# Layer 0 of a two-layer transformer block: biases in one piece, experts' first tokens loaded three waves ahead, small steps moved into gaps, copies behind products

## The chip, the cores and the metric

The kernel runs on one core of a Trainium2 chip. Its engines work from queues of their own and meet only through semaphores: TensorE (PE, matrix products and transposes, with a separate track for loading weights, PEld), VectorE (DVE), ScalarE (ACT), GpSimd (POOL) and SyncE (SP, which here only issues DMA transfers). DMA transfers are also issued from ACT's and POOL's queues. The metric is the device time of one execution in microseconds; the number compared is the median of the runs.

## What is computed

The input x has 8 sequences of 512 tokens with 256 features, in float32. Two layers follow each other.

```python
x = layernorm(x + attention0(x))      # 16 heads of 16, softmax over keys j >= i
x = layernorm(x + experts0(x))        # 8 experts, top 2; the last one only scales x;
                                      # 7 have 256 -> 1024 -> relu -> 256, at most 512 tokens each
x = layernorm(x + attention1(x))      # RMS norm, rotary positions, sigmoid weights
x = layernorm(x + experts1(x))        # 8 experts 256 -> 512 -> silu -> 256, and 4 that only scale x; top 2
```

Each query, key and value is a product of x with a 256x256 matrix plus a bias. Experts of layer 0 take the first 512 tokens that chose them, in the order of the tokens.

## The kernel before, in words

The kernel keeps all sequences in SBUF (`own[b]`, 128 partitions x 4 x 256) and writes one instruction stream by hand. Inside `tc.manual_schedule()` the order of the source is the order on each engine; outside it, as in `layer0()`, where weights and constants are loaded, a scheduler places the instructions.

**Start.** `layer0()` loads the first sequence, the query and key weights (`unspread`, L262, pieces of 16 floats), and the two biases. A bias of 256 numbers comes from the host as 128 x 4, where only 16 of every 32 partitions hold data. `packed` (L254) brings it into the layout of the products, 128 x 2, with eight small DMA transfers; the query's eight go out on SP's queue and the key's eight on ACT's queue. DVE then builds `bq_t` and `bk_t` (L400 to L402). `turned_in(0, kc)` (L466, L469) transposes the first sequence on PE in two halves, with one copy on ACT after each. Both halves use the one PSUM buffer that `bank()` gives in this layer, so the second half's transposes wait for the first copy. `query` (L499, L506) then multiplies by the weights.

**Waves.** `waves0(start, stop)` runs attention in steps called waves, 16 for each sequence. Each wave computes scores of four heads for one block of keys, their exponentials on ACT, a mask on POOL, and the products with the values; beside these it runs the small steps that `beside0` lists for that wave, for the sequence before and the one after. In the waves of sequence 6 the rows of sequence 4 are scattered into `xbuf`, two of the last eight in each of waves 8 to 11 (L764, indirect DMA on POOL's queue). Only sequences 0 to 4 are scattered here; a flag says later whether experts had room left, and a second pass follows if so.

**Experts of layer 0.** After the 112 waves of sequences 0 to 6, `experts0` runs the seven experts, and then the waves of the last sequence follow. Two experts' weights are loaded long before. `tokens0(e)` (L1333, SP's queue) loads an expert's 512 rows from `xbuf` into a tile of the pool tag "e", which has five buffers and also holds the exponentials of the waves. `turn(e)` (L1350) transposes them into a two-bank PSUM tile of `wide()`, of which there are three, and DVE and ACT copy one half each (L1354, L1355). Four groups of products follow (L1368), each with a relu copy on ACT or DVE, then four output blocks of eight products (L1385). All four blocks lie in one PSUM tile of two banks; after the second block DVE copies the first bank (L1392), after the fourth ACT copies the second (L1394). Then SP stores the result and loads weights and tokens of expert e+2.

**Steps in gaps.** 37 small steps of attention are left at that point: four transposes back to token order of sequence 6 (`by_token`, L589, with a reciprocal and a multiplication on DVE, L595 and L598), four query or key products of sequence 7 (`query`), then `by_feature`, `kept`, `projected` and the routing. They stand in a list; `gap()` runs the next one. Before the first `turn(0)` eight are run in a row, four `by_token` and four `query` in turn, all through the single buffer of `bank()`. The rest are run in the gaps of the experts, of which there are seven for each expert and six for the last.

Of the kernel before, what the change touches and what calls it, by code (L numbers as in the profile page):

```python
# [9 lines left out]
FP = mybir.dt.float32  # L10
# [7 lines left out]
P = 128  # L18
B, S, D = 8, 512, 256
NT = B * S  # L20
KC = D // P
NC = S // P
NH, HD = 16, 16
NHS = 4
# [19 lines left out]
def tile_two_layers(  # L44
# [33 lines left out]
    nc = tc.nc  # L78
# [5 lines left out]
    p = {}  # L84
# [11 lines left out]
    def bank():  # L96
        return p["mm"].tile([P, 512], FP, tag="mm", name="mm")


    ident = const.tile([P, P], FP, name="ident")  # L100
# [6 lines left out]
        out=before, in_=ones, pattern=[[1, P]], compare_op=ALU.is_gt, fill=0.0,  # L107
# [35 lines left out]
    for i, (seqs, always) in enumerate(LOTS):  # L143
        n = seqs * S
        lot = SimpleNamespace(
            i=i, first=len(lot_of), n=n, slots=E1 * n, always=always, most=2 * n // TB + E1 - 1
# [97 lines left out]
    def packed(pool, src, n, name, queue=nc.sync):  # L244

        t = pool.tile([P, KC, n], FP, name=name)
        unspread_rows(t, src, queue)
        return t
# [9 lines left out]
    def unspread(pool, src, name, queue=nc.sync):  # L258

        t = pool.tile([P, KC, NH, HD], FP, name=name)  # L260
        for kc in range(KC):
            queue.dma_start(  # L262
                out=t[:, kc],
                in_=src[kc * P : (kc + 1) * P, :].rearrange("p (h x) -> p h x", x=32)[:, :, :HD],
            )
        return t.rearrange("p k h x -> p k (h x)")
# [78 lines left out]
    att = work.enter_context(tc.tile_pool(name="att", bufs=1))  # L345
    alone = ExitStack()
    wp = alone.enter_context(tc.tile_pool(name="w0", bufs=1))
# [10 lines left out]
    def pair(name):  # L358
        return att.tile([P, 2, S], FP, tag="e", name=name, bufs=5)

    def layer0():
        def load_x(b):
            nc.sync.dma_start(out=own[b], in_=x[b].rearrange("(c p) d -> p c d", p=P))

        st = [{} for _ in range(B)]
        load_x(0)
        wq_s = unspread(wp, wq0, "wq_s")
        wk_s = unspread(wp, wk0, "wk_s", nc.scalar)
        bq_s = packed(wp, bq0.unsqueeze(2), 1, "bq_s")
        bk_s = packed(wp, bk0.unsqueeze(2), 1, "bk_s", nc.scalar)  # L370

        wv_s = wp.tile([P, KC, D + 8], FP, name="wv_s")
        nc.sync.dma_start(out=wv_s[:, :, :D], in_=wv0.rearrange("(k p) f -> p k f", p=P))
# [25 lines left out]
        for m in range(KC):  # L399
# [9 lines left out]
            out=shade[:, :P], in_=shade[:, :P], pattern=[[1, P]], compare_op=ALU.is_ge, fill=MASKED,  # L409
# [882 lines left out]
    def waves0(start, stop):  # L1292
        nonlocal waiting
        t = l0
        for g in range(start, stop):
            b, w = g // 16, g % 16
            now = None
            if g >= 0:
                now = t.scores(b, w // 8, w // 4 % 2, NC - 1 - w % 4)
                if w % 4 == 0:  # L1300
                    t.fill(b, w // 4)
                if w == 10 and b + 2 < B:
                    t.load_x(b + 2)
            if (g + 2) % 4 == 0 and 0 <= g + 2 < 16 * B:
                ob, ow = (g + 2) // 16, (g + 2) % 16
                t.lowered(ob, ow // 8, ow // 4 % 2)
            first, second = beside0(b, w if g >= 0 else g)
            if b == 0 and w in (1, 3, 4, 5, 8, 9):
                fn, arg = t.rsteps.pop(0)
                fn(arg)  # L1310
            if b == 2 and w < len(l1.steps):
                fn, arg = l1.steps[w]
                fn(arg)
            run(first)
            ob, ow = (g + AHEAD) // 16, (g + AHEAD) % 16
            if ob < B:
                t.greatest(ob, ow // 8, ow // 4 % 2, (1, 0, 3, 2)[ow % 4])
            if waiting:
                t.gathered(*waiting)
            run(second)  # L1320
            waiting = now
# [6 lines left out]
        nc.sync.dma_start(out=wo, in_=we_out[e].rearrange("(f p) d -> p f d", p=P))  # L1328
        return wi, wo

    def tokens0(e):
        xe = pair(f"xe{e}").rearrange("p u (c d) -> p (u c) d", d=D)
        nc.sync.dma_start(  # L1333
            out=xe, in_=xbuf[e * CAP : (e + 1) * CAP, :].rearrange("(c p) d -> p c d", p=P)
        )
        return xe

    def experts0(loaded, h, steps):

        xes = {e: tokens0(e) for e in range(2)}  # L1340

        def gap():
            if steps:
                run([steps.pop(0)])

        def turn(e):
            ps = wide()
            for kc in range(KC):
                for c in range(NC):
                    nc.tensor.transpose(  # L1350
                        ps[:, kc, c * P : (c + 1) * P], xes[e][:, c, kc * P : (kc + 1) * P], ident
                    )
            xeT = pair(f"xeT{e}")
            nc.vector.tensor_copy(xeT[:, 0, :], ps[:, 0, :])  # L1354
            nc.scalar.copy(xeT[:, 1, :], ps[:, 1, :])  # L1355
            return xeT

        for _ in range(8):
            gap()
        xeT = turn(0)  # L1360
        for e in range(E0):
            wi, wo = loaded[e]
            for f2 in range(I0 // P // 2):
                ps = wide()
                for u in range(2):
                    f = 2 * f2 + u
                    for kc in range(KC):
                        nc.tensor.matmul(  # L1368
                            out=ps[:, u, :], lhsT=wi[:, kc, f * P : (f + 1) * P], rhs=xeT[:, kc, :],
                            start=(kc == 0), stop=(kc == KC - 1),  # L1370
                        )
                for u in range(2):
                    if f2 % 2 == 0:
                        nc.scalar.activation(h[2 * f2 + u], ps[:, u, :], AF.Relu)
                    else:
                        nc.vector.tensor_scalar(h[2 * f2 + u], ps[:, u, :], 0.0, None, ALU.max)
                gap()
            if e + 1 < E0:
                xeT = turn(e + 1)
                gap()  # L1380
            ps = wide().rearrange("p u (c d) -> p (u c) d", d=D)
            ye = pair(f"ye{e}").rearrange("p u (c d) -> p (u c) d", d=D)
            for c in range(NC):
                for f in range(I0 // P):
                    nc.tensor.matmul(  # L1385
                        out=ps[:, c, :], lhsT=h[f][:, c * P : (c + 1) * P], rhs=wo[:, f, :],
                        start=(f == 0), stop=(f == I0 // P - 1),
                    )
                if c % 2 == 0:
                    gap()  # L1390
                elif c == 1:
                    nc.vector.tensor_copy(ye[:, :2, :], ps[:, :2, :])  # L1392
                else:
                    nc.scalar.copy(ye[:, 2:, :], ps[:, 2:, :])  # L1394
            nc.sync.dma_start(
                out=ybuf[e * CAP : (e + 1) * CAP, :].rearrange("(c p) d -> p c d", p=P), in_=ye
            )
            if e + 2 < E0:
                loaded[e + 2] = weights0(e + 2)
                xes[e + 2] = tokens0(e + 2)  # L1400
        run(steps)
# [128 lines left out]
    loaded = {}  # L1530
    with tc.manual_schedule():
        for kc in range(KC):
            l0.turned_in(0, kc)
        for which in ("q", "k"):
            for part in range(2):
                l0.query(0, 0, which, part, lambda: wide()[:, 0, :])
        waves0(-AHEAD, 32)
        l1 = layer1(att.tile([P, KC, S], FP, tag="aoT", name="turns"))
        waves0(32, 48)
        for e in range(2):  # L1540
            loaded[e] = weights0(e)
        waves0(48, 16 * (B - 2))
        h = [half(f"h{f}") for f in range(I0 // P)]
        waves0(16 * (B - 2), 16 * (B - 1))
        l0.gathered(*waiting)
        waiting = None
        a, z, n = B - 2, B - 3, B - 1
        t = l0
        steps = [(t.by_token, a, 0), (t.query, n, 1, "q", 0), (t.by_token, a, 1), (t.query, n, 1, "q", 1)]
        steps += [(t.by_token, a, 2), (t.query, n, 1, "k", 0), (t.by_token, a, 3), (t.query, n, 1, "k", 1)]  # L1550
        steps += [(t.by_feature, a, kc) for kc in range(KC)]
        steps += [(t.kept, z, c) for c in (2, 3)]
        steps += [(t.projected, a, c) for c in range(NC)]
        steps += [(fn, z) for fn in (t.chosen, t.raised, t.shared, t.pointed, t.counted)]
        steps += [(t.filled,)]
        steps += [(fn, z) for fn in (t.ranked, t.sent)]
        steps += [(fn, a) for fn in (t.normed, t.logits)]
        steps += [(t.kept, a, c) for c in range(NC)]
        steps += [
            (fn, a) for fn in (t.chosen, t.raised, t.shared, t.pointed, t.counted, t.ranked, t.sent)  # L1560
        ]
        experts0(loaded, h, steps)
    moe0.close()
    planp = ctx.enter_context(tc.tile_pool(name="planp", bufs=1, side="right"))
    rows1 = ExitStack()
# [432 lines left out]
```

## Time and profile before

| | |
|---|---|
| median of 3 runs | 1585.18 us (1585.05 to 1585.28) |
| profiled execution | 1617.07 us, its span 1615.4 us |
| mean granted TensorE clock | 0.944 |
| busy in the span | PE 1456.2 us, DVE 903.9, ACT 675.9, POOL 479.5 |
| first query product | at 15.49 us |
| last products of the 112 waves | end at 571.2 us |
| first `turn(0)` transpose, first expert product | 593.93 us, 596.70 us |
| last expert product | ends at 808.2 us |

The profile is that of one execution, which was 2.0% longer than the median of the runs. In its lines a time is the start in microseconds from the beginning of the span, followed by the duration; the bracket at the end says how long the engine had been idle before and what released it. "SPq" and "ACTq" are DMA issues of these engines' queues. A float32 product appears as two PE records, a transpose as one. Some PE records are missing from the trace, so counts there are a lower bound.

### The profile page before, as it was taken

Reading aid. Unit: us, or ns where it says so; the run is one execution under the profiler, and the core shown is the slowest. Engines: PE = TensorE matmul, PEld = TensorE weight load, DVE = VectorE, ACT = ScalarE, POOL = GpSimd, SP = SyncE. Lnnn points to the kernel's source line nnn. Section 1 sums busy time; section 2 is a strip of 40 time slices with the busy share of each in tenths; the row PEclk is TensorE's granted clock in tenths of the full one; section 3 lists DMA queues with packets and bytes.
Section 4 is the critical chain, followed back from the end, with each engine's and each line's share of the span. In section 5 each row is a group of like instructions: output and inputs, shape, how many; then the busy total and the mean of one; then the engine's idle time right before and its main releaser. Section 6 shows DMA issues by size and latency. Waiting matters only on the chain. (4 is left out here: it accounts for less than half of the span.)

```text
span 1615.4 us, 24867 instructions
## 1 busy us (share of the span) xinstructions
PE 1456.2 (90%) x8558; PEld 773.1 (48%) x8558; DVE 903.9 (56%) x3443; ACT 675.9 (42%) x1001; POOL 479.5 (30%) x602
## 2 busy tenths in 40 slices
PE   5999889898989879999998999999999999999992
PEld 3444444444443336666633333333333333778882
DVE  3655667676767532321073656767767665453394
ACT  2544444453544321111043655656665656222242
POOL 2221233232323300000044303435445422432453
PEclk8999999999999979999988988999998999999996
DMA  8949950000000002233010001022012004557774
GB/s 194 284 142 356 355 168 15 10 15 12 13 12 11 4 27 78 79 115 119 13 47 21 27 2 27 26 27 39 26 25 42 19 3 132 173 170 233 260 241 155
DMA packets 136364, 150.01 MB, mean 93 GB/s; under 512 B 29869, under 2 KB 119242, under 8 KB 136226
## 3 DMA queue, kind: packets, MB, share of 16 engines
q1 hardware_dynamic: 118242, 121.63, 24.0%
q0 software_dynamic: 10560, 23.51, 5.8%
q10 hardware_dynamic: 7424, 3.15, 0.8%
q8 instruction: 72, 1.18, 0.3%
q14 instruction: 66, 0.54, 0.1%
HBM read 77.01 MB, written 77.10 MB: 95 GB/s over the span
## 5 line engine op out<-in xcount | busy, mean ns | idle before, releaser
L967 ACT ACTIVATE e<-sc 128x1024 f32<-128x1024 f32 x256 | 248.8, 1022 | 163.0 <-PE sc L959 150.6
L561 POOL TENSOR_SCALAR_AFFINE_SELECT e<-e 128x256 f32<-128x256 f32 x256 | 103.8, 413 | 629.2 <-ACT e L558 626.6
L530 DVE CUSTOM_DVE_ANT_0 seen<-sc,shade 128x128 f32<-128x128 f32 (+3 forms) x512 | 250.7, 490 | 62.0 <-PE sc L522 32.9
L558 ACT ACTIVATE e<-sc 128x1024 f32<-128x1024 f32 (+3 forms) x256 | 168.8, 702 | 99.0 <-PE sc L549 88.7
L549 PE MATMUL sc<-q,k 32*128 32x512 f32 (+3 forms) x1024 | 137.2, 506 | 10.9 <-DVE mpad L530 9.9
L976 PE MATMUL av<-e,v 128*32 128x512 f32 x1024 | 143.8, 634 | 0.0
L522 PE MATMUL sc<-k,q 32*128 32x384 f32 (+3 forms) x1024 | 131.4, 514 | 9.5 <-ACT e L558 5.0
L573 PE MATMUL av<-e,v 128*32 128x512 f32 (+3 forms) x1024 | 101.6, 467 | 4.0 <-POOL e L561 3.6
L1385 PE MATMUL sc<-wo,h 128*128 128x256 f32 x448 | 100.5, 381 | 4.8 <-DVE ye L1392 4.8
L1677 PE MATMUL yp<-w_e,h 128*128 128x256 f32 x416 | 96.5, 384 | 3.0 <-DVE h L1669 2.1
L1368 PE MATMUL sc<-xeT,wi 128*128 128x512 f32 x224 | 98.1, 593 | 0.9 <-DVE xeT L1354 0.9
L1661 PE MATMUL sc<-xtT,w_e 128*128 128x256 f32 x416 | 94.3, 380 | 0.3 <-issue 0.3
L1385 PEld LDWEIGHTS sc<-wo,h 128*128 128x128 f32 x448 | 84.0, 190 | 19.3 <-DVE ye L1392 7.9
L959 PE MATMUL sc<-q,k 16*128 16x512 f32 x512 | 84.3, 668 | 6.7 <-ACT e L967 3.2
L549 PEld LDWEIGHTS sc<-q,k 32*128 32x128 f32 x1024 | 52.7, 190 | 73.8 <-issue 42.7
L1677 PEld LDWEIGHTS yp<-w_e,h 128*128 128x128 f32 x416 | 79.7, 193 | 14.9 <-DVE h L1669 2.5
L1688 POOL DMA_INDIRECT ybuf<-yt,to x52 | 51.0, 980 | 114.5 <-DVE yt L1687 103.4
L959 PE MATMUL sc<-q,kb 32*128 32x512 f32 x512 | 80.6, 649 | 4.6 <-ACT e L967 4.6
L1661 PEld LDWEIGHTS sc<-xtT,w_e 128*128 128x128 f32 x416 | 77.2, 190 | 10.1 <-issue 0.5
L522 PEld LDWEIGHTS sc<-k,q 32*128 32x128 f32 x1024 | 53.8, 195 | 54.1 <-issue 21.1
L1142 POOL DMA_INDIRECT xbuf<-x,idx x64 | 68.0, 1062 | 23.8 <-issue 15.5
L506 ACT ACTIVATE q<-mm,bq_t,lanes 128x256 f32<-128x256 f32 x60 | 30.6, 561 | 103.1 <-PE mm L499 103.1
(287 smaller groups left out, 2166.6 us busy)
## 6 DMA issues: line engine op xcount, KB each, us to landing
xbuf<-blank SPq DMA_DIRECT2D x130, 272.0 KB
w_e<-in_w SPq DMA_DIRECT2D x104, 256.0 KB
ybuf<-blank SPq DMA_DIRECT2D x16, 512.0 KB
y<-ybuf SPq DMA_DIRECT2D x16, 512.0 KB
wi<-in_we_in SPq DMA_DIRECT2D x7, 1024.0 KB
wo<-in_we_out SPq DMA_DIRECT2D x7, 1024.0 KB
xt<-xbuf SPq DMA_DIRECT2D x26, 272.0 KB
own<-in_x SPq DMA_DIRECT2D x8, 512.0 KB
```

The source lines that it names most:

```text
L522: nc.tensor.matmul(out=places[r], lhsT=q["q", m, t][32 * r : 32 * r + 32, ib * P : (ib + 1) * P], rhs=q["k", m, t][32 * r : 32 * r + 32, i ...
L530: nc.vector.tensor_tensor_reduce(out=seen[:, :width], in0=places[r], in1=shade[:, :width], scale=-1.0, scalar=-MASKED, op0=ALU.add, op1=AL ...
L549: nc.tensor.matmul(out=places[r], lhsT=q["k", m, t][32 * r : 32 * r + 32, jb * P : (jb + 1) * P], rhs=q["q", m, t][32 * r : 32 * r + 32, : ...
L558: nc.scalar.activation(e[:, :, :width], s[:, :, :width], AF.Exp, scale=SCALE)
L561: nc.gpsimd.affine_select(out=own, in_=own, pattern=[[0, 2], [-1, P]], compare_op=ALU.is_ge, fill=0.0, base=0, channel_multiplier=1,)
L573: nc.tensor.matmul(out=q["av"][32 * r : 32 * r + 32, : (jb + 1) * P], lhsT=vs[b % 2][:, jb, 8 * m + 2 * r + t, :], rhs=es[r], start=(jb == ...
L959: nc.tensor.matmul(out=scs[r // 2][:, r % 2, :], lhsT=k[32 * r : 32 * r + lanes, jb * P : (jb + 1) * P], rhs=q["q", m][32 * r : 32 * r + l ...
L967: nc.scalar.activation(e, scs[pr], AF.Sigmoid, scale=SCALE)
L976: nc.tensor.matmul(out=q["av"][32 * r : 32 * r + 32, :], lhsT=vs[b % 2][:, jb, 8 * m + 2 * r + t, :], rhs=es[r // 2][:, r % 2, :], start=( ...
L1385: nc.tensor.matmul(out=ps[:, c, :], lhsT=h[f][:, c * P : (c + 1) * P], rhs=wo[:, f, :], start=(f == 0), stop=(f == I0 // P - 1),)
L1661: nc.tensor.matmul(out=ps[:, f // 2, f % 2 * TB : (f % 2 + 1) * TB], lhsT=q.wi[kc][:, f * P : (f + 1) * P], rhs=q.xtT[:, kc, :], start=(kc ...
L1677: nc.tensor.matmul(out=q.ps[c], lhsT=q.h[:, f // 2, at : at + P], rhs=q.wo[f // 2][:, f % 2 * D : (f % 2 + 1) * D], start=(f == 0), stop=( ...
```

## The change

Four things are changed, all in layer 0.

1. The two biases are each loaded with one DMA transfer on SP's queue, as they come (128 x 4), into `spread`. DVE copies the right columns of the identity matrix into `lane`, and two products on PE with `lane` as weights put the numbers in the layout of the products. DVE copies the result from PSUM to `biases`. The eight DMA transfers on SP's queue and the eight on ACT's queue are gone. The order that the scheduler gives puts the two new products at the head of PE's queue, ahead of the first transposes, and they use the buffer of `bank()` that the transposes need next; on SP's queue the two loads stand between the first sequence and the query weights.
2. The first two experts' tokens are loaded three waves before the end of sequence 6, into one tile of the tag "o" (two buffers), instead of after the last wave into two tiles of the tag "e".
3. `turn(0)` comes first; then two steps instead of eight are run before the first expert; the other 35 go into the 48 gaps.
4. Both copies of an expert's output stand behind all four blocks of products.

```diff
         load_x(0)
+        spread = wp.tile([P, 2, NHS], FP, name="spread")
+        for i, src in enumerate((bq0, bk0)):
+            nc.sync.dma_start(out=spread[:, i, :], in_=src)
+        wk_s = unspread(wp, wk0, "wk_s", nc.scalar)
         wq_s = unspread(wp, wq0, "wq_s")
-        wk_s = unspread(wp, wk0, "wk_s", nc.scalar)
-        bq_s = packed(wp, bq0.unsqueeze(2), 1, "bq_s")
-        bk_s = packed(wp, bk0.unsqueeze(2), 1, "bk_s", nc.scalar)
+        lane = wp.tile([P, NHS, HD], FP, name="lane")
+        nc.vector.tensor_copy(lane, ident.rearrange("p (g x) -> p g x", x=32)[:, :, :HD])
+
+        ps = bank()[:, : 2 * KC].rearrange("p (i m) -> p i m", m=KC)
+        for a in range(2):
+            nc.tensor.matmul(
+                out=ps[64 * a : 64 * a + 64],
+                lhsT=lane.rearrange("p g x -> p (g x)"),
+                rhs=spread.rearrange("p i (m a) -> p i m a", a=2)[:, :, :, a],
+                start=True, stop=True,
+            )
+        biases = wp.tile([P, 2, KC, 1], FP, name="biases")
+        nc.vector.tensor_copy(biases.rearrange("p i m o -> p i (m o)"), ps)
+        bq_s, bk_s = biases[:, 0], biases[:, 1]
...
-    def tokens0(e):
-        xe = pair(f"xe{e}").rearrange("p u (c d) -> p (u c) d", d=D)
+    def tokens0(e, xe=None):
+        if xe is None:
+            xe = pair(f"xe{e}").rearrange("p u (c d) -> p (u c) d", d=D)
...
-    def experts0(loaded, h, steps):
-
-        xes = {e: tokens0(e) for e in range(2)}
+    def experts0(loaded, xes, h, steps):
...
-        for _ in range(8):
+        xeT = turn(0)
+        for _ in range(2):
             gap()
-        xeT = turn(0)
...
                 if c % 2 == 0:
                     gap()
-                elif c == 1:
-                    nc.vector.tensor_copy(ye[:, :2, :], ps[:, :2, :])
-                else:
-                    nc.scalar.copy(ye[:, 2:, :], ps[:, 2:, :])
+            nc.vector.tensor_copy(ye[:, :2, :], ps[:, :2, :])
+            nc.scalar.copy(ye[:, 2:, :], ps[:, 2:, :])
...
-        waves0(16 * (B - 2), 16 * (B - 1))
+        waves0(16 * (B - 2), 16 * (B - 1) - 3)
+
+        xe = att.tile([P, 2, 2, S], FP, tag="o", name="xe", bufs=2)
+        xes = {
+            e: tokens0(e, xe[:, e].rearrange("p u (c d) -> p (u c) d", d=D)) for e in range(2)
+        }
+        waves0(16 * (B - 1) - 3, 16 * (B - 1))
...
-        experts0(loaded, h, steps)
+        experts0(loaded, xes, h, steps)
```

## The prediction

> **What bounds the kernel now.** I read the page's busy times first: PE is busy for 90% of the span, the next engine for 56%.
>
> ```profile
> PE 1456.2 (90%) x8558; PEld 773.1 (48%) x8558; DVE 903.9 (56%) x3443; ACT 675.9 (42%) x1001; POOL 479.5 (30%) x602
> ```
>
> So PE's idle time is what can be won, and any PE work added where PE is busy is paid in full. Next the timeline of the start (start, duration, engine, line).
>
> ```profile
> 4.88 9.03 ACTq L254 DMA_DIRECT2D bk_s<-in_bk  x8
> 5.50 1.09 PE L466 MATMUL mm<-ident,own 128*128 128x128 f32 x4 [5.50 <-DMA own<-in_x]
> 5.76 8.48 SPq L254 DMA_DIRECT2D bq_s<-in_bq  x8
> 13.95 0.59 ACT L469 COPY xT<-mm 128x512 f32<-128x512 f32 x1 [11.86 <-DMA bk_s<-in_bk]
> 14.59 1.12 PE L466 MATMUL mm<-ident,own 128*128 128x128 f32 x4 [8.00 <-ACT xT L469]
> 15.49 3.81 PE L499 MATMUL sc<-xT,wq_s 128*128 128x256 f32 x8
> 15.74 0.59 ACT L469 COPY xT<-mm 128x512 f32<-128x512 f32 x1 [1.21 <-PE mm L466]
> ```
>
> The first transposes are done at 6.6, but ACT, which must copy them, is issuing the key bias's eight transfers until 13.9. The second copy ends at 16.33, and only then can query products be completed. The DMA view of 8 to 12 us (40 slices of 0.1 us) tells when the weights are there at the latest:
>
> ```profile
> DMA  8989999999999999922220000000000000110000
> ```
>
> The engines are full until 9.7 us. Now the hand-over to the experts, from the timeline of 571 to 600 us:
>
> ```profile
> 576.58 2.04 PE L499 MATMUL mm<-xT,wq_s 128*128 128x256 f32 x4 [3.01 <-DVE ao L598]
> 578.66 1.02 ACT L506 ACTIVATE q<-mm,bq_t,lanes 128x256 f32<-128x256 f32 x2 [5.47 <-PE mm L499]
> 579.74 1.11 PE L589 MATMUL mm<-ident,o 128*128 128x128 f32 x4 [1.11 <-ACT q L506]
> 581.75 2.04 PE L499 MATMUL mm<-xT,wq_s 128*128 128x256 f32 x4 [0.90 <-DVE ao L598]
> ...
> 593.93 1.92 PE L1350 MATMUL sc<-ident,xe 128*128 128x128 f32 x8
> 596.70 3.70 PE L1368 MATMUL sc<-xeT,wi 128*128 128x512 f32 x8 [0.85 <-DVE xeT L1354]
> ```
>
> Eight steps go through one PSUM buffer, product, copy, product, copy, at half clock: the table by stage has 12.23 us of PE in the 22 us from 572 to 594, at a granted clock of 0.58, against 39.15 of 40 at 1.00 from 600 to 640. Last, the output blocks, where PE waits for DVE's copy of a bank that it has finished:
>
> ```profile
> 617.53 3.62 PE L1385 MATMUL sc<-wo,h 128*128 128x256 f32 x16
> 621.25 0.69 DVE L1392 COPY ye<-sc 128x512 f32<-128x512 f32 x1 [2.42 <-PE sc L1385]
> 621.99 3.72 PE L1385 MATMUL sc<-wo,h 128*128 128x256 f32 x16 [0.85 <-DVE ye L1392]
> ```
>
> And SP's waits, for the tokens:
>
> ```profile
> SPq L1333 <- DMA xbuf<-own,idx_all: 340.5, 1, 340.5
> SPq L1333 <- PE av L573: 11.8, 2, 8.7
> ```
>
> **What the Trainium skill says.** "TensorE: Matmul & The Clock Gate", section "What's actually happening": the array falls to half clock after an idle window of about 3.4 us and returns after about as long of sustained work. The trace agrees: the query of two products (four records) takes 2.04 us in the stretch above and 1.13 at 544.24. "DMA: Bandwidth & Descriptors", section "Issuing engines are not separate DMA queues": transfers from SP and ACT share the same engines, so moving biases from ACT's queue saves issue time only; the trace agrees, in that both weights, one on each queue, share the engines until about 9.7 us. The same page, section "Queues, rings and completion order": each engine consumes a queue's descriptors in ring order; so the bias loads, issued right behind the first sequence and ahead of the query weights, need not wait for these. No run here shows it yet.
>
> **Part 1, the start.** Removed: eight issues (9.03 us) from ACT's queue, eight (8.48 us) from SP's. Added on SP: two issues, 0.43 each by the nearest row (bo_c, 128x2, at 17.20), which put the query weights' issue 0.9 later, hidden because their data waits behind the first sequence's. Now PE's head waits for the biases. The first sequence was there at 5.50; I take 5.9 for the biases (bounds 5.5, in the same breath, and 7.5, some 2 us behind). Two tiny products 0.3 (estimate from 0.27 for one transpose), DVE's copy 0.15 (as the 128x8 copy L491), hand-overs 0.25: 6.6. Transposes 1.09, copy 0.59, transposes 1.12, copy 0.59 and four hand-overs of some 0.03 to 0.1: 10.2. The weights: full engines until 9.7, of which the removed small loads were part, plus 0.7 for the semaphore: 10.4 (bounds 9.7 and 11.5). The later of the two decides: 10.4 instead of 16.4, **6.0 us** (bounds 4.9 and 6.4). The lane copy on DVE (0.15) runs while DVE is idle. Is something else late then? The value bias was issued at 16.18 and needed at 22.01; it moves to about 11.1 (SP was held by the query weights until 8.8) and is needed at 16. The zero fills behind it start 5 to 6 earlier as well, so they meet the same waves.
>
> **Part 2, tokens early.** The last scatter had arrived at 567.44 - 8.7 = 558.7; from there SP waited only for buffers of tag "e". In the new place both loads go out at once, with nothing else on SP's queue until the first expert's store. The old load's data moved from 568.4 to 570.6, so `turn(0)` at 571.3 would have found its tokens anyway within a microsecond: this part alone I price at 0 (bounds 0 and 1); what it does is let part 3 be safe.
>
> **Part 3, steps in gaps.** Wave products end at 571.2. `turn(0)` takes 1.04 at full clock (the row at 611.42), `by_token` stands behind it. DVE is late: its queue of maxima and logits ends at 575.73; then xeT 0.69, reciprocal and multiplication 0.74, so the query starts at about 577.3 (576.58 before, plus 0.69), half clock, 2.04: 579.3. Expert 0's products follow at once. They start cold: 1.4 lost (bounds 0 and 3.4), against 0.27 lost before (3.70 against 3.43). So 596.97 becomes 580.7: 16.3 won. Paid back: six steps now stand in PE's full stream. Four transposes there cost 0.44 (the next product after 604.11 starts at 604.55), a query 0.87 (four records; 16 records of 256 columns take 3.45): 3 x 0.44 + 3 x 0.87 = 3.9. One hand-over is tight: `by_token` right behind `turn(1)`, about 0.3, since ACT needs 1.02 for the query's copy and `turn(1)` covers 1.0. Elsewhere 3.4 us of products cover each copy. 35 steps fit in 48 gaps. **12.1 us** (bounds 9 and 14). The flag that SP reads moves to the sixth gap of expert 2; SP needs it before that expert's store, and PE needs nothing from SP for 20 us after.
>
> **Part 4, copies.** 617.53 + 3.45 = 620.98 is when the third block could start; it starts at 621.99: 1.0 for each of seven experts, **7.1 us** (5.9 by the wait of 0.85, 7.9 by PEld's waits). DVE's copy now runs beside ACT's; the PSUM tile is needed again two product groups later, 7 us, so nothing waits; the store is 0.1 later at the most.
>
> **Sum.** 6.0 + 12.1 + 7.1 = 25.2 us of the span of 1615.4. The profiled execution (1617.07) is 2.0% longer than the median, so I scale by 0.98: 24.7, and 1585.2 - 24.7 = **1560.5**. After 808 us PE stays the bound, with no wait for a DMA in the list, so the shift should last to the end.
>
> **Rivals.**
> - *The start gives nothing* (weights or biases land late, or the time is lost to fills): 19.2 x 0.98 = 18.8, 1566.4. For it: the weights' landing is inferred. Against it: DMA is quiet after 10 us. Chance 0.13.
> - *Steps stall in the gaps* as they do now: six times the 0.9 to 1.1 of the rows above, about 6: 1566.4. For it: still one buffer. Against it: 3.4 us of cover. Chance 0.10.
> - *More is won*: half clock shortened. From 29.9 to 41 us products also run at double length (2.13, 2.07); if the earlier start spares that stretch, some 6 more, and the cold 1.4: 1553. Chance 0.12.
> - *Slower: the clock.* If PE's new rhythm made it fall to half clock where it is now full, each cold microsecond costs half. To end slower by 0.2% it must lose 28 us, 56 us of extra half clock, four times the stretch at the start; in the experts the profile shows 1.00 throughout. 1590, chance 0.03.
> - *Nothing*: a wait behind the experts absorbs all, 1585. No such wait is in the list. Chance 0.02.
>
> **How the numbers follow.** The forecast itself has 0.60, with its own range of 1556 to 1565 from the bounds. The range of 8 in 10 reaches to the neighbours: 1553 to 1568. A difference within 0.2% (3.2 us) could not be told from none: faster 0.95, the same 0.02, slower 0.03.
>
> **What would show it.** ACT's first copy near 7.7 and complete query products near 10.4, no longer 16.4; the first expert product at 573 to 574 in the new span (579.3 less 6.0), no eight steps ahead; no wait of L1400 for DVE's copy; the distance from the first expert product to the last (211.5 before) about 3 shorter: 7.1 won, 4.2 paid back. Wrong would be: PE's head waiting past 8 us, gaps with idle PE in expert 0, or half clock in the experts.

## The result

The changed kernel takes 1562.2 us (median of 4 runs, 1560.8 to 1563.08), the kernel before 1585.23 (4 runs). The ratio is 0.9861, with a 95% interval of 0.9847 to 0.9875: 23.0 us or 1.4% faster. Forecast were 1560.5 us, 24.7 faster.

On the page after, the first part says that PE is the bound as before. Its busy time is shorter than the 1456.2 us of the first profile before, but most of that is a long layer 1 in that profile; a second profile of the kernel before (below) has 1432.3:

```profile
PE 1427.1 (92%) x8562; PEld 765.6 (49%) x8562; DVE 908.3 (58%) x3445; ACT 675.9 (43%) x1001; POOL 479.0 (31%) x602
```

The timeline of the start, PE's lines and then ACT's (start, duration, engine, line, and in brackets the idle time before and its releaser):

```profile
6.91 0.38 PE L377 MATMUL mm<-spread,lane 128*64 128x4 f32 x4 [6.91 <-DMA spread<-in_bk]
7.59 1.09 PE L481 MATMUL mm<-ident,own 128*128 128x128 f32 x4 [0.30 <-POOL mpad L431]
9.35 1.12 PE L481 MATMUL mm<-ident,own 128*128 128x128 f32 x4 [0.68 <-ACT xT L484]
10.26 3.81 PE L514 MATMUL sc<-xT,wq_s 128*128 128x256 f32 x8
...
8.71 0.59 ACT L484 COPY xT<-mm 128x512 f32<-128x512 f32 x1 [6.62 <-PE mm L481]
10.50 0.58 ACT L484 COPY xT<-mm 128x512 f32<-128x512 f32 x1 [1.21 <-PE mm L481]
```

PE now waits for the biases at its head, until 6.91. ACT copies as soon as PE is done, and the second copy ends at 11.08 instead of 16.33. (The bracket at 7.59 names a POOL memset that ends at 7.57, but the wait is for DVE's copy of the biases out of the same PSUM buffer, which ends at 7.49: in p1_biases below, the memset ends at 7.57 again, the copy at 7.59, and the transposes start at 7.70, so they follow the copy by about 0.1 us in both.)

PE's timeline from the last wave products into the first expert, and then an expert's output blocks:

```profile
566.38 0.86 PE L588 MATMUL av<-e,v 128*32 128x256 f32 x16
567.17 1.09 PE L1365 MATMUL sc<-ident,xe 128*128 128x128 f32 x8
...
573.24 2.04 PE L514 MATMUL mm<-xT,wq_s 128*128 128x256 f32 x4 [3.60 <-DVE ao L613]
575.07 5.22 PE L1383 MATMUL sc<-xeT,wi 128*128 128x512 f32 x8
580.13 0.60 PE L604 MATMUL mm<-ident,o 128*128 128x128 f32 x4
...
599.13 7.07 PE L1400 MATMUL sc<-wo,h 128*128 128x256 f32 x32
```

The chain of eight steps is gone; one wait of 3.60 is left in which DVE finishes its maxima. The first expert's eight products take 5.22 instead of 3.70, since about half of them run at half clock. The second and third output block are one uninterrupted row of 32 records; before, DVE's copy stood between them.

Where the time went can be laid out along four places that all kernels have. The last copy of attention output of sequence 6 marks the end of the waves; from there to the last expert product is the experts' stretch. A second profile of the kernel before (below) is used, because the first one had a long layer 1.

| | before, again | after |
|---|---|---|
| query products can be completed | 16.2 us | 11.1 us |
| second copy of attention output (sequence 0) | 79.52 | 71.76 |
| end of the waves | 572.24 | 568.69 |
| last expert product | 807.84 | 785.78 |
| experts' stretch | 235.6 | 217.1 |

So the start gives 5 to 8 us, of which some 4 are left at the end of the waves, and the experts' stretch gives 18.5.

### The profile page after: what moved, and what is told of

Same layout as the page of the kernel before. It is cut to its first block, busy times and chain, and to the rows that moved or that the text cites. A ratio compares the mean times of both kernels' runs of the same rounds, so it can differ in the third digit from the quotient of the medians.

```text
span 1559.6 us, 24858 instructions
## 1 busy us (share of the span) xinstructions
PE 1427.1 (92%) x8562; PEld 765.6 (49%) x8562; DVE 908.3 (58%) x3445; ACT 675.9 (43%) x1001; POOL 479.0 (31%) x602
## 5 line engine op out<-in xcount | busy, mean ns | idle before, releaser
L991 PE MATMUL av<-e,v 128*32 128x512 f32 x1024 | 138.3, 612 | 0.0
L974 PE MATMUL sc<-q,k 16*128 16x512 f32 x512 | 79.1, 659 | 3.9 <-PEq L1600 2.3
L974 PE MATMUL sc<-q,kb 32*128 32x512 f32 x512 | 77.3, 640 | 0.4 <-ACT e L982 0.4
```

Of the source, the lines that this page charges most:

```text
L974: nc.tensor.matmul(out=scs[r // 2][:, r % 2, :], lhsT=k[32 * r : 32 * r + lanes, jb * P : (jb + 1) * P], rhs=q["q", m][32 * r : 32 * r + l ...
L991: nc.tensor.matmul(out=q["av"][32 * r : 32 * r + 32, :], lhsT=vs[b % 2][:, jb, 8 * m + 2 * r + t, :], rhs=es[r // 2][:, r % 2, :], start=( ...
```

## The experiments

In all of them the ratio is to the kernel before, run on the same chip.

**The kernel before once more.** No edit. The spans of the first profiles before and after differ by 55.8 us while the medians differ by 23.0, so one of them isn't typical.

> The kernel before, unchanged, profiled once more, because its first profile (1617.07 us) lies 32 us above its runs. Theory (the change acts in layer 0 alone): this execution is near 1585 us, the experts' stretch from the end of the wave products to the last expert product is again 237 us, and layer 1's waves, 400 us in the first profile, take about 375 as in the changed kernel, because those 25 us were half clock in that one execution. Rival (the change shortens layer 1 too): layer 1's waves take about 400 us again.

It took 1582.69 us. The first and last score product of layer 1 are seen in the list of the instructions of that line, in the first profile and in the second (minimum, median and maximum duration in ns, then first and last start in us):

```profile
L959 PE MATMUL sc<-q,k x512: 587/692/1218, 871.6 to 1361.8; 16*128 16x512 f32 x171
```

```profile
L959 PE MATMUL sc<-q,k x512: 587/692/1218, 871.2 to 1332.6; 16*128 16x512 f32 x171
```

Up to layer 1 both are alike within 0.5 us; then the first needs 490.2 us, the second 461.4, as the changed kernel does (461.6). Of the 34.4 us between the two spans these waves of layer 1 make 28.8 (about 25 were expected), and most of the rest comes behind them; the change has no part in them. The clock accounts for most of it: in these stretches PE was busy for 469.2 and 447.9 us with the same 2746 records, at a granted clock of 0.94 and 0.98. The experts' stretch is 235.6, close to the 237 expected.

**Each part alone.** From the kernel before, one part of the diff each.

```diff
# p1_biases: only the loads, the two products and the copy of the biases
# p2_tokens: only waves0(..., 16 * (B - 1) - 3), the tile of the tag "o", and tokens0(e, xe)
# p3_steps
-        for _ in range(8):
+        xeT = turn(0)
+        for _ in range(2):
             gap()
-        xeT = turn(0)
# p4_copies
                 if c % 2 == 0:
                     gap()
-                elif c == 1:
-                    nc.vector.tensor_copy(ye[:, :2, :], ps[:, :2, :])
-                else:
-                    nc.scalar.copy(ye[:, 2:, :], ps[:, 2:, :])
+            nc.vector.tensor_copy(ye[:, :2, :], ps[:, :2, :])
+            nc.scalar.copy(ye[:, 2:, :], ps[:, 2:, :])
```

> Part 1 alone: biases loaded in one piece each and ordered by two products; all else as before. Theory (the start's gain stays): 6 us faster than before, 1579; complete query products at about 11.1 us instead of 16.4. The changed kernel stood 8.0 us ahead at the first sequence's end and 3.9 ahead at the end of the wave products; theory: that is the clock's coming and going, so here the lead at the end of the waves may be anything from 3 to 9 and PE's granted clock in the waves explains the difference. Rival (the waves give the start's gain back, fills and loads meeting them at a worse place): 4 us or less, and the lead falls between 150 and 571 us at the same waves at the same granted clock.

> Part 2 alone: the first two experts' tokens loaded three waves earlier, in a tile of the tag o; eight steps ahead of the experts, biases and copies as before. Theory: worth nothing, within 1 us of before, 1584, because turn(0) comes more than 20 us after the old load has landed; the loads go out near 559 us and land long before. Rival (the buffers that the old load held, or the scatter just ahead, cost something): 2 us or more, either way.

> Part 3 alone: turn(0) first, two steps ahead of the first expert instead of eight, 35 in gaps; tokens are loaded where they were before. Theory (the token load is early enough as it was): 12 us faster than before, 1573, and turn(0) waits less than 1 us for its tokens. Rival (the early load is what makes it possible): turn(0) waits for the tokens 2 us or more, and 9 us or less are won.

> Part 4 alone: both copies of an expert's output behind all four blocks. Theory: 1.0 us for each of seven experts, 7 us faster than before, 1578; no wait of the third block for DVE. Rival (PE's wait was only moved, to the next expert's products or to the store and its buffers): 2 us or less.

| kernel | median, us | ratio (95%) | experts' stretch, us |
|---|---|---|---|
| p1_biases | 1580.74 | 0.998 (0.997 to 0.999) | 235.6 |
| p2_tokens | 1583.79 | 0.9997 (0.9987 to 1.0006) | 235.6 |
| p3_steps | 1573.47 | 0.9936 (0.9918 to 0.9954) | 224.8 |
| p4_copies | 1577.06 | 0.9960 (0.9946 to 0.9973) | 228.0 |
| all four (after) | 1562.2 | 0.9861 (0.9847 to 0.9875) | 217.1 |

Part 2 is worth nothing, as priced. Part 3 shortens the stretch by 10.8, part 4 by 7.6, and together they shorten it by 18.4 to 18.5: they add up without touching each other. Whether the tokens come in time without part 2 is seen in p3_steps, PE's timeline:

```profile
569.48 1.07 PE L1350 MATMUL sc<-ident,xe 128*128 128x128 f32 x8 [0.17 <-DMA xe<-xbuf]
```

It waits 0.17 us for the old load. The rival, that the early load is what makes part 3 possible, falls; in this kernel the load was early enough. There was no time to spare, though, and turn_early (below), which starts this transposition at 562.33, rests on the early load.

Part 1 alone gives 0.2% or about 3.2 us over 22 runs, although its second copy ends 5.0 us earlier. In its profile the lead over the second profile before is 4.9 at the second copy of attention output and 5.0 at the end of the waves, so this one execution shows nothing given back. The time is the rival's, 4 us or less, but the sign named with it is missing. The runs list their mean granted clock: it is 0.9536 for these 22 and 0.9545 for the 28 of the kernel before. That is about 1.4 us of full clock, enough for most of the missing 1.8, but not clear of noise.

**The whole once more, and without part 1.** The second is the changed kernel with the old loads of the biases.

> The changed kernel, unchanged, once more, to have it beside the next two on one chip. Theory (the parts add up: 5.0 for the start, 10.8 and 7.6 in the experts' stretch, as the profiles of the single parts showed): 23 us faster than before, 1561; the experts' stretch again 217 us; the lead at the end of the first sequence 5 or 8 us and that at the end of the waves 3 to 8, as the clock falls. Rival (the parts help each other): the stretch stays at 217, but the start's lead is 8 us each time.

> The changed kernel without part 1: biases loaded as before. Theory (the experts' stretch is 18.4 us shorter whatever the start does; of the start's 5 to 6 us only about 4 reach the end of the waves, because PE spends more of the waves at half clock): 18 to 19 us faster than before, so 4 slower than the changed kernel, and the experts' stretch is again 217 us. Rival (the start's whole lead lasts): 6 us slower than the changed kernel.

The whole: 1561.56, ratio 0.9854 (0.9838 to 0.9871); its profile leads by 5.8 us at the second copy of attention output and by 2.7 at the end of the waves, a little less than the 3 to 8 expected. Without part 1: ratio 0.9858 (0.9822 to 0.9894), on a chip where the kernel before took 1597.08, so that it can't be told by the time from the whole. (The three profiles from that chip are 785 to 791 us long behind the last expert product, the others 773 to 777, the first one before apart. The kernels don't differ there, and the cause is open.) Its stretch is 217.3, as that of the whole. For the start I take all eleven profiles of kernels with the first version of either start (the later version below apart):

| | second copy of attention output | end of the waves |
|---|---|---|
| six with the old biases, mean (range) | 78.8 (76.4 to 81.8) | 572.1 (570.1 to 574.4) |
| five with the new, mean (range) | 72.9 (71.2 to 74.6) | 568.5 (567.3 to 569.6) |
| lead | 5.8 | 3.6 |

So the start wins 5.8 us on average, and 3.6 reach the end of the waves, which agrees with the 3.2 of the runs. Where the rest goes can be read from the table by stage. First p1_biases, then the kernel before, then the changed kernel, each from its second copy of attention output to the end of its waves (stretch, its length, busy PE, PEld, DVE, ACT, POOL with their numbers of records, granted clock, DMA share, GB/s):

```profile
74.58:567.26 492.68, 436.89 (x3215) 207.39 (x3215) 322.58 (x1382) 220.02 (x380) 139.78 (x257) 0.95 0.28 92
```

```profile
79.52:572.24 492.72, 436.81 (x3215) 207.44 (x3215) 323.01 (x1382) 220.03 (x379) 139.85 (x257) 0.95 0.29 92
```

```profile
71.76:568.69 496.93, 443.05 (x3223) 210.70 (x3223) 323.21 (x1382) 220.16 (x379) 139.20 (x257) 0.94 0.29 93
```

The instruction streams are the same here but for eight records in the third, which are `turn(0)`, about 1 us. DVE, ACT and the DMA engines are busy for as long in all three; PE is busy 6.2 us longer in the third, at a clock of 0.94 against 0.95. In the trace's record of the granted clock PE is at half clock for 44.4 us of each of the first two stretches and for 58.0 of the third. It comes in periods of 3.41 us or whole multiples of it, and the more of them, the longer the waves: 492.7 us with 13 in these two, 495.8 with 15 in after_again, 496.9 with 17 here and 498.0 with 18 in no_gap_first. So the loss of 4.2 us is PE at half clock, not fills or loads that meet the waves at a worse place.

Why some executions get more of these periods was not tested. An earlier start as such is not enough: p1_biases lost nothing, and the three profiles of the later version below, which start earlier still, lead the mean of the old start by 7.1 us at the second copy of attention output and by 7.0 at the end of the waves.

**What is left of the stall.** Two kernels go on from the changed one: no step ahead of the first expert, and `turn(0)` ahead of the last wave.

```diff
# no_gap_first
         xeT = turn(0)
-        for _ in range(2):
-            gap()
# turn_early: as no_gap_first, with turn(0) moved out of experts0
-        waves0(16 * (B - 1) - 3, 16 * (B - 1))
+        waves0(16 * (B - 1) - 3, 16 * (B - 1) - 1)
+        xeT0 = turned0(0, xes[0], dve=False)      # turn(0), both halves copied by ACT
+        waves0(16 * (B - 1) - 1, 16 * (B - 1))
```

> The changed kernel with no step ahead of the first expert: all 37 go into the 48 gaps. Theory (the query ahead of the first expert costs 2.04 us at half clock, in a gap 0.87; the transposes are free where they stand and 0.44 in a gap): 1 us faster than the changed kernel, first expert product 2.5 us earlier against the end of the waves. Rival (half clock simply moves on to the first products): no difference.

> The changed kernel with turn(0) ahead of the last wave of sequence 6, both halves copied on ACT, and no step ahead of the first expert. Theory (what remains of the stall is DVE's backlog of maxima, 4.5 us, and the half clock that PE's idleness there brings): 6 us faster than the changed kernel, 1555; the first expert product follows the last wave product within 1 us at full clock. Rival (the backlog only comes due elsewhere: the PSUM tiles of maxima are held by DVE, and the second product group waits for them; or the last wave is slowed by ACT's two copies): 2 us or less.

Without the two steps: 1562.29, ratio 0.9867 (0.9852 to 0.9882), no difference from the whole that the runs can tell. PE's timeline, no_gap_first and then turn_early:

```profile
573.04 6.58 PE L1381 MATMUL sc<-xeT,wi 128*128 128x512 f32 x8 [4.26 <-DVE xeT L1369]
579.46 0.60 PE L604 MATMUL mm<-ident,o 128*128 128x128 f32 x4
```

```profile
562.33 1.09 PE L1358 MATMUL sc<-ident,xe 128*128 128x128 f32 x8
...
566.70 0.86 PE L588 MATMUL av<-e,v 128*32 128x256 f32 x16
567.49 3.70 PE L1387 MATMUL sc<-xeT,wi 128*128 128x512 f32 x8
```

The first products start earlier, but nearly all of the eight run at half clock, 6.42 us until the next instruction. The table by stage shows what became of the stretch at half clock, which in the kernel before is 20.5 us long (575.5 to 596.0). Here are the changed kernel and no_gap_first, each over that stretch, and turn_early from its first to its last expert product (columns as above; the third number from the end is the granted clock):

```profile
571.50:578.35 6.85, 5.11 (x8) 2.86 (x9) 1.52 (x5) 1.60 (x3) 0.00 (x0) 0.50 0.00 0
```

```profile
572.05:578.90 6.85, 5.86 (x7) 2.52 (x8) 0.90 (x3) 0.59 (x1) 0.00 (x0) 0.50 0.00 0
```

```profile
567.49:777.05 209.56, 209.32 (x794) 142.18 (x790) 50.56 (x184) 31.47 (x61) 0.00 (x0) 1.00 0.24 78
```

Removing the two steps leaves the stretch at half clock as long as it was, 6.85 us; it only covers other work. The rival holds; the stretch is 0.9 us shorter in the trace, which the time can't show. With the tokens turned before the last wave, the first expert follows the last wave product at full clock. That kernel takes 1554.28 us, ratio 0.9821 (0.9808 to 0.9835), 7.3 us less than the whole beside it, and its stretch is 209.1, shorter by 8.0. DVE's backlog is still there; nothing waits for it any more.

**The start, again.** The two bias products are emitted after the eight transposes, into a PSUM tile of `wide()`; and this joined to turn_early.

```diff
# biases_behind
-        ps = bank()[:, : 2 * KC].rearrange("p (i m) -> p i m", m=KC)
-        ...                                   # products, copy, bq_t and bk_t, placed by the scheduler
+        def biased():
+            ps = wide()[:, 0, : 2 * KC].rearrange("p (i m) -> p i m", m=KC)
+            ...                               # the same
...
         for kc in range(KC):
             l0.turned_in(0, kc)
+        l0.biased()
```

> The changed kernel with the two bias products behind the first eight transposes on PE, in a PSUM tile of wide(). Theory (PE's head waited 1.4 us for the biases, and the transposes then for the copy out of their buffer): the first transposes start at 5.5 instead of 7.6 us, the second copy ends near 9.1 instead of 11.1, and the query products are complete 1 to 2 us earlier, unless the weights land later than 9.1; the time 0 to 2 us less than the changed kernel's, which the clock's wandering may hide. Rival (the weights land near 10.3 at the earliest): query products start at 10.3 as before, waiting for the weights, and nothing is won beyond 0.8.

> turn(0) ahead of the last wave, no step ahead of the first expert, and the bias products behind the transposes. Theory: the 8 us of the early turn, and up to 1 us for the biases: 1553 to 1554. Rival (the two disturb each other): 1556 or more.

> The kernel with both improvements once more, because the chip of its first run had the kernel before 12 us slower than elsewhere and the runs wide apart. Theory (8 us for the early turn and about 1.2 for the weights being the limit at the start): a ratio of 0.980 to 0.982 to the kernel before, complete query products near 10 us, first expert product within 1 us of the last wave product. Rival (the first run's ratio of 0.979 was that chip's): 0.982 or more, no better than the early turn alone.

biases_behind, PE's timeline:

```profile
8.25 1.22 PE L515 MATMUL sc<-xT,wq_s 128*128 128x256 f32 x2
9.88 2.90 PE L515 MATMUL sc<-xT,wq_s 128*128 128x256 f32 x6 [0.41 <-DMA wq_s<-in_wq]
```

Now the second half of the query weights is the limit: it is there at 9.88, so the query products are complete 1.2 us earlier than in the changed kernel. Its ratio is 0.9817 (0.9782 to 0.9853), on the chip of without_p1; the interval touches that of the whole. Both together: 0.979 (0.9753 to 0.9827) there, and 0.9841 (0.9816 to 0.9866), 1554.54 us, in the second run. The second run's ratio is the rival's: no better than the early turn alone. The version that is faster than both kernels clear of noise, on one chip, is turn_early; what 1.2 us at the start add to it is below what these runs can tell.

## Why the prediction was right, point by point

- **The start, 6.0 us.** The mechanism held: ACT's queue was what kept the transposes waiting. The size was a little off, in two terms. The biases were there at 6.91, not at 5.9 (inside the bounds), and since they stand at PE's head, all behind them moved by as much: the second copy ended at 11.1, not 10.2. The weights, said to be the limit at 10.4, were there at 9.88, as biases_behind shows; the 0.7 put down for the semaphore had no line behind it. The gain until query products can be completed is 5.3 us between the first profiles, and 5.8 on average at the second copy of attention output.
- **That the shift lasts to the end.** This step failed in part: 3.6 of 5.8 us reach the end of the waves, and the runs give part 1 alone 3.2. The list of waits had no DMA in it, and but for one of 0.25 us in the experts (below) none came. What the list doesn't show is that the same instructions can take longer: PE's own half clock.
- **Tokens early, 0.** Right: 0.9997, and turn(0) would have waited 0.17 us without it.
- **Steps in gaps, 12.1 us.** 10.8 were won. The distance from the end of the waves to the first expert product fell from 24.1 to 6.4, 17.7 against 17.4 forecast. The clock took 1.64 more from the first eight products in p3_steps (5.18 against 3.54 until the next instruction), 1.1 being in the sum. The six steps in the full stream cost what they were priced at: in the changed kernel the query at 584.01 is followed at 584.87, the transposes at 588.30 at 588.74. The tight place was where it was expected: `by_token` behind `turn(1)` waits 0.24 and costs 0.90 in all, 0.46 above its price, where 0.3 was put down. "Elsewhere 3.4 us of products cover each copy" was wrong in two places. A `projected` now stands right behind `turn(2)`, with only that turn between it and the one before, and costs about 0.36 more. And `ranked` of sequence 6 comes one output block (3.45 us) after `counted`, whose counts it needs, where before two blocks (6.9) lay between. DVE has to finish `pointed` and the copy of the turned tokens first; in after_again the counts are there at 720.04, 0.84 after that block, and the expert with it is 0.57 longer than its moved products explain. In the first profile after, 0.42 of the same loss comes earlier: `turn(5)` starts at 714.36 after waiting for its tokens, whose load was issued at 703.80; these loads have little time to spare.
- **The sign "about 3 shorter".** From the first expert product to the last it is only 0.8 shorter (210.7 against 211.5). The 1.1 of cold products, which the sum had, was left out of this sign; the rest is the larger loss at half clock and the three tight places.
- **Copies, 7.1 us.** 7.6 in the stretch of p4_copies; the distance between experts without steps on PE fell from 29.48 to 28.42, 1.06 for each.
- **The scale of 0.98.** It had no ground: the first profile wasn't 2% longer everywhere, it was long in layer 1. On a sum of 25 it made 0.5, in the right direction by luck. By the profiles the parts gave 3.6, 10.8 and 7.6 us, together 22.0, where 6.0, 12.1 and 7.1 had been forecast.
- **The rivals.** "Steps stall in the gaps" and "the clock" are each true in small: about 1.4 us (0.46, 0.36 and 0.57 at the tight places) and 2.2 (5.8 less 3.6). "More is won": on some executions the stretch at half clock that began near 30 us was shorter (3.4 us instead of 13.7 in the first profile after, which gave it a lead of 8.0 us at the second copy of attention output), but this was lost again in the waves, and p3_steps and without_p1 had it too (6.8 and 3.4 us) with the old start.

## What to carry to other kernels

Where an engine's queue has a row of tiny DMA issues ahead of a copy that another engine waits for, their issue time, not their bytes, is the cost; here eight issues held ACT for 9 us. Small serial steps belong between long products, but count the distance between each step and the one it needs, for gaps aren't equal. And look at what keeps PE idle just before a long stretch: here the idle time was paid again at half clock, and moving the one transposition that the stretch needs ahead of the last wave was worth more than taking steps away.

## What the runs showed of the hardware

- Two executions of one kernel can differ by PE's clock: in the first profile before, layer 1's waves took 490 us instead of 461 with the same instructions, at a granted clock of 0.94 instead of 0.98.
- A gain ahead of a long stretch that PE bounds needn't arrive whole, execution by execution: on average 5.8 us became 3.6, with PE's busy time rising where DVE's and ACT's stayed. Half clock came in periods of 3.41 us, and each one more made the waves about 1 to 1.5 us longer.
- Idle times of 3.0 to 4.3 us on PE went with half clock for the work behind them: the first query after 3.01 us in the kernel before, for about 5 us from 573.24 in the changed kernel after 3.60, for about 6 us from 573.04 in no_gap_first after 4.26. The gaps of about 1 us that DVE's copies made between output blocks left the clock full (3.72 for 16 records, against 3.62).
